# A transformer layer with a routed feed-forward: the shared expert's gate and up products as seven half-size products

## The chip, the cores and the metric

The kernel runs on one core of a Trainium2 chip. A core has five engines with queues of their own: TensorE (PE, matrix products into PSUM), VectorE (DVE), ScalarE (ACT), GpSimd (POOL) and SyncE (SP, which issues most transfers). They meet at semaphores. The metric is the device time of one execution in microseconds, the median of several runs.

## The reference

The input is 2 x 2048 tokens of width 512, treated as 4096 rows. Three blocks follow one another: an attention against two fixed weight matrices, a cross attention to 128 context rows, and a feed-forward with one shared expert and 32 routed experts, of which each token takes one. The change is in the shared expert:

```python
def _swiglu(x, gw, uw, dw):
    return jax.nn.silu(x @ gw) * (x @ uw) @ dw
...
x = hidden_states.reshape(-1, h)
shared_out = _swiglu(x, shared_gate_w, shared_up_w, shared_down_w)
logits = x @ gate_w
topk_ids = jnp.argmax(logits, axis=-1)
...
d = _grouped_mm(jax.nn.silu(g) * u, routed_down_w, tokens_per_expert)
inv = jnp.argsort(order)
routed_out = d[inv]
return (shared_out + routed_out).reshape(b, s, h)
```

Here `x` is 4096 x 512 (normalised rows), the gate and up weights are 512 x 1024, the down weights 1024 x 512.

## The kernel before

Products of fp32 precision are made of three passes on TensorE. `split` (line 88) cuts a value into a high half (a cast, line 93, on ScalarE unless told otherwise) and a low half (what is left, line 96, on VectorE or GpSimd), and `three` (line 162) gives the three pairs low-high, high-low and high-high. One product of a 128-row contraction is so three matmuls, each with its own weight load.

The stages follow in program order: `stage0` (attention), `stage1` (cross attention; its `finish` writes the sum x2, the normalised and transposed rows as high and low halves into the DRAM tensor `zT`, the gate logits and the scaled rows `xs`), `shared`, `routed`, and `overflow`, a loop for tokens that exceed the planned capacities. A scheduler orders each engine's instructions by priority (program order unless `later` moves it) and by a model of the times; tiles of one tag share a fixed number of slots, and a tile waits for a free one. Stages overlap where tiles and data allow.

`shared` works on tiles of 512 tokens (`t`, 8 of them) and on six of the eight blocks of 128 hidden columns (`HID`). `up(t, c)` makes gate and up of one block, 12 matmuls of 512 columns each (4 contraction blocks times 3) into one bank of PSUM each, then Silu on ScalarE, the product on VectorE, and the split of the hidden value. `down(t)` makes 4 x 6 x 3 = 72 matmuls into four banks, adds x2 and writes `out`; it is issued after the first block of the next tile. The weights of all six blocks are loaded and split once, by `shared_weights`, in the background of stage 1's end, and stay in 36 of the 48 slots of the pool W. The last two hidden blocks, called rest, have their own 12 slots and are worked in `routed` by `Rest`, in 16 blocks of 256 tokens between the experts' blocks.

`route` (called once, after the first tile) computes on VectorE which token goes to which expert's rows, and scatters the token numbers into the DRAM list `ids` with 32 indirect transfers from GpSimd's queue (line 719), each of which writes the same tensor and so waits for the one before it. Line 721 then reads the list back; `gather` in `routed` needs it.

`routed` loads each expert's gate, up and down weights (lines 897, 898), splits them into slots of W (gate and up, 16 + 16) and of the tags A and B (down), and works blocks of 256, 128 or 64 tokens.

Of the kernel before, what the change touches and what calls it, by code (L numbers as in the profile page):

```python
# [14 lines left out]
A = mybir.AluOpType  # L15
# [22 lines left out]
HID = 6  # L38
# [6 lines left out]
class Ctx:  # L45


    SLOTS = {"A": 8, "B": 8, "C": 5, "D": 4, "E": 4, "F": 8, "G": 4, "H": 3, "I": 2, "J": 2, "K": 2}

    def __init__(self, tc, stack):  # L50
        self.tc, self.nc = tc, tc.nc
        enter = stack.enter_context
        self.c = enter(tc.tile_pool(name="c", bufs=1))
        self.sm = enter(tc.tile_pool(name="sm", bufs=3))
        self.raw = enter(tc.tile_pool(name="raw", bufs=6))
        self.W = enter(tc.tile_pool(name="W", bufs=48))
        self.a = enter(tc.tile_pool(name="a", bufs=1))
        self.ps = enter(tc.tile_pool(name="ps", bufs=2, space=PSUM))
# [301 lines left out]
def stage1(g, x1, mask, kst, vst, gate, x2, zT, xs, ef, background):  # L360
# [143 lines left out]
    def finish(t):  # L504
# [13 lines left out]
        for i, v in enumerate(z):  # L518
            normalise(g, v[:], v[:], mv, rs, i)
        yield  # L520
        z2 = transposed(z, "z", "BBEF" if t < NT - 2 else "JJKK")
        for i in range(2):
            for c in range(2):
                nc.sync.dma_start(zT[i, :, 2 * c:2 * c + 2, t * 256:(t + 1) * 256], f32(z2[i][c][:]))
# [79 lines left out]
def route(g, ef, tab, tri, ids, plan, idx):  # L604
# [34 lines left out]


    oh = table("oh", bc(io, 1, E), bc(ef[:], 2, E), A.is_equal, tag="J")
    pos, cnt = ([g.tile("G", n, F32, (128, 16, E)) for _ in range(2)] for n in ("pos", "cnt"))
    for hf in range(2):
        for w, dst in ((0, pos), (1, cnt)):
# [3 lines left out]
            V.tensor_copy(dst[hf][:], o[:])  # L648
    for t in range(1, E):
# [3 lines left out]
        V.tensor_tensor(cnt[h][:, i, :], cnt[h][:, i, :], cnt[hp][:, ip, :], A.add)  # L653


# [4 lines left out]
    total(rank[:], table("gt", bc(key[:], 1, E), bc(key[:], 2, E), A.is_gt)[:])  # L660
    ro = table("ro", bc(io, 1, E), bc(rank[:], 2, E), A.is_equal, tag="J")
    base, cap, er = small("base"), small("cap"), small("er")
    total(base[:], table("wb", ro[:], bc(basec, 1, E), A.mult)[:])
    total(cap[:], table("wc", ro[:], bc(capc, 1, E), A.mult)[:])
    total(er[:], table("we", ro[:].rearrange("p e r -> p r e"), bc(io, 1, E), A.mult)[:])
    V.tensor_copy(plan[:, 0:E], er[:])


# [7 lines left out]
    V.tensor_copy(plan[:, 96:97], nov[:])  # L676
    ovs, ove = small("ovs"), small("ove")
    total(ovs[:], table("lt", bc(io, 2, E), bc(io, 1, E), A.is_gt, bc(over[:], 1, E), A.mult)[:])
    V.tensor_tensor(ove[:], ovs[:], over[:], A.add)
    for hf in range(2):  # L680
        te = small(f"te{hf}")
        total(te[:], table("le", bc(iota[:, 32 * hf:32 * hf + 32], 2, E), bc(ove[:], 1, E), A.is_ge)[:])
        V.tensor_scalar(te[:], te[:], float(E - 1), None, A.min)
        V.tensor_copy(plan[:, 32 + 32 * hf:64 + 32 * hf], te[:])


# [3 lines left out]
    for hf in range(2):  # L690
# [4 lines left out]
        past = g.tile("K", "past", F32, (128, 16, E))  # L695
        V.tensor_tensor(sel[:], pos[hf][:], capb, A.is_ge)
        V.tensor_tensor(past[:], sel[:], capb, A.mult)
        V.tensor_tensor(pos[hf][:], pos[hf][:], past[:], A.subtract)
        V.tensor_tensor(sel[:], sel[:], diffb, A.mult)
        V.tensor_tensor(sel[:], sel[:], baseb, A.add)  # L700
        V.tensor_tensor(sel[:], sel[:], oh[:, ts, :], A.mult)
        total(blk[:, ts], sel[:])
        V.tensor_tensor(pos[hf][:], pos[hf][:], oh[:, ts, :], A.mult)
        total(pt[:, ts], pos[hf][:])
    pi, hi = small("pi", I32), small("hi", I32)
# [7 lines left out]
    V.tensor_tensor(blk[:], blk[:], pt[:], A.add)  # L713
    dst, toki = small("dst", I32), small("toki", I32)
    V.tensor_copy(dst[:], blk[:])
    V.tensor_copy(toki[:], tok)
    flat = ids[:].rearrange("p (b o) -> (p b) o", o=1)
# [7 lines left out]
def shared_weights(g, wg, wu, wd):  # L725

    g.sw, g.rest = {}, {}
# [8 lines left out]
    g.sw["d"] = yield from weight_steps(g, wd[0:768, :], 6, 512, "sd")  # L736
    for name, w in (("g", wg), ("u", wu)):
# [4 lines left out]
        yield from split_steps(g, w[:, 768:1024], *o)  # L742
    g.rest["d"] = yield from weight_steps(g, wd[768:1024, :], 2, 512, "rd")


def shared(g, zT, x2, out, routing, rest):
    nc = g.nc
    NT = T // 512
    wg2, wu2, wd2 = (g.sw[z] for z in "gud")
    H = {}  # L750

    def up(t, c, z):
        o = []
        for nm, w2, tag in (("g", wg2, "P3"), ("u", wu2, "P2")):
            p = g.bank(tag, nm)
            n = 0
            for k in range(4):
                for w, y in three((w2, z)):
                    nc.tensor.matmul(p[:], part(w, k, c), y[k][:], start=n == 0, stop=n == 11)
                    n += 1  # L760
            o.append(p)
        s = g.tile("H", "s")
        nc.scalar.activation(s[:], o[0][:], AF.Silu)
        nc.vector.tensor_tensor(s[:], o[1][:], s[:], A.mult)  # L764
        hh, hl = g.tile("A", "hh", FR), g.tile("B", "hl", FR)
        split(g, hh[:], hl[:], s[:])
        H[t, c] = (hh, hl)

    def down(t):
        o = [g.bank(("P4", "P1")[s // 2], "d") for s in range(4)]  # L770
        for c in range(HID):
            h2 = H.pop((t, c))
            for s in range(4):
                for n, (w, y) in enumerate(three((wd2, h2))):
                    nc.tensor.matmul(o[s][:], y[:, s * 128:(s + 1) * 128], w[c][0], start=c == 0 and n == 0, stop=c == HID - 1 and n == 2)
        for s in range(4):
            rows = slice(t * 512 + s * 128, t * 512 + s * 128 + 128)
            b = g.tile("I", "b")
            nc.sync.dma_start(b[:], x2[rows, :])
            nc.vector.tensor_tensor(b[:], o[s][:], b[:], A.add)  # L780
            nc.sync.dma_start(out[rows, :], b[:])

    for t in range(NT):
        z = []
        for i in range(2):
            tag = ("EF", "CD")[t % 2][i]
            z.append([g.tile(tag, f"z{i}", FR) for _ in range(4)])
# [469 lines left out]
```

## Time and profile before

| | us |
|---|---|
| median of 3 runs | 2712.58 (2712.46 to 2713.4) |
| the profiled execution | 2710.05 |
| its span | 2708.3 |
| first matmul of the shared stage (line 759) | 1402.7 |
| last matmul of the shared stage (line 775) | 1819.8 |
| first matmuls of the rest and routed stage (line 827) | 1820.0 |

The span runs from the first to the last record of the profiled execution, and times in the views count from its start. The share of an engine's busy time is over the whole span. Matmuls overlap one another, and their ends are modelled, so the sum of their lengths is not time. The mean transfer rate per fortieth of the span lies between 32 and 191 GB/s up to the end of the shared stage and between 268 and 330 GB/s in most of the routed one.

### The profile page before, as it was taken

What the parts mean: (1) busy time and instruction counts of PE and PEld (TensorE: products, weight loads), DVE (VectorE), ACT (ScalarE), POOL (GpSimd) and SP (SyncE); (2) the same over time, 40 slices, a digit from 0 to 9 for tenths busy, and PEclk for the clock granted to TensorE, in tenths of its full rate; (3) what the DMA queues carried; (4) which work ended last, traced back from release to release, by engine and by line L of the source; (5) the groups of instructions that cost most, each with busy time, mean ns of one, the idle gap of its engine ahead of it and who ended that gap; (6) DMA issues with size and microseconds to landing.
All of it is one profiled execution on the core that took longest, in us unless ns stands there. A gap on an engine that the chain in (4) does not pass through costs nothing. (4 is left out here: it accounts for less than half of the span.)

```text
span 2708.3 us, 46790 instructions
## 1 busy us (share of the span) xinstructions
PE 2658.4 (98%) x14736; PEld 2293.1 (85%) x14736; DVE 1960.8 (72%) x4605; ACT 1802.8 (67%) x4012; POOL 953.9 (35%) x788
## 2 busy tenths in 40 slices
PE   7999999999999999999999999999999999999998
PEld 5878888887888999899988888888989898888886
DVE  7777777777777988888876722243777777778995
ACT  6788787888767777777774111133666777767884
POOL 5576565666643333333330130001122111212221
PEclk9999999999999999999999999999999999999999
DMA  4012122212121223222245323254888999999994
GB/s 151 32 63 83 59 67 80 77 43 82 34 82 33 80 76 114 95 88 79 85 145 191 98 94 106 86 170 113 268 281 277 287 300 292 300 276 287 330 325 130
DMA packets 237995, 396.64 MB, mean 146 GB/s; under 512 B 29377, under 2 KB 67281, under 8 KB 237745
## 3 DMA queue, kind: packets, MB, share of 16 engines
q1 hardware_dynamic: 223024, 366.45, 40.3%
q0 software_dynamic: 14720, 27.19, 5.1%
q8 instruction: 116, 1.90, 0.3%
q14 instruction: 135, 1.10, 0.1%
HBM read 311.67 MB, written 83.83 MB: 146 GB/s over the span
## 5 line engine op out<-in xcount | busy, mean ns | idle before, releaser
L96 DVE TENSOR_TENSOR rl<-raw,rh 128x512 fp32r<-128x512 f32 x768 | 488.6, 684 | 101.5 <-ACT rh L93 94.5
L93 ACT CAST rh<-raw 128x512 fp32r<-128x512 f32 x768 | 439.2, 621 | 121.9 <-DMA raw<-in_rg 76.5
L96 POOL TENSOR_TENSOR pl<-p,ph 128x512 fp32r<-128x512 f32 x320 | 411.0, 1295 | 269.7 <-ACT ph L93 217.0
L343 ACT ACTIVATE rl<-s 128x512 f32<-128x512 f32 x512 | 293.1, 604 | 39.5 <-PE s L339 33.6
L1043 POOL DMA_INDIRECT out_dram<-v,idx x46 | 100.5, 2185 | 430.0 <-ACT v L1041 352.2
L347 DVE TENSOR_TENSOR p<-s,rl 128x512 f32<-128x512 f32 x320 | 215.2, 683 | 41.7 <-ACT rl L343 39.3
L93 ACT CAST ph<-p 128x512 fp32r<-128x512 f32 x320 | 199.2, 626 | 63.6 <-DVE p L347 60.7
L452 ACT ACTIVATE e<-e,nm 128x128 f32<-128x128 f32 x512 | 199.2, 391 | 61.5 <-DVE nm L449 61.3
L455 POOL TENSOR_TENSOR e<-e,ri 128x512 f32<-128x512 f32 x128 | 133.5, 1043 | 243.7 <-DVE ri L453 126.5
L339 PE MATMUL s<-qh,kwl 128*128 128x512 f32 x512 | 205.7, 403 | 8.0 <-DVE p L347 4.0
L303 PE MATMUL o<-pl,vwh 128*128 128x512 f32 x512 | 202.4, 395 | 0.5 <-POOL pl L96 0.5
L303 PE MATMUL o<-ph,vwl 128*128 128x512 f32 x512 | 200.4, 393 | 0.9 <-ACT ph L93 0.9
L339 PE MATMUL s<-ql,kwh 128*128 128x512 f32 x512 | 200.4, 391 | 0.0
L339 PE MATMUL s<-qh,kwh 128*128 128x512 f32 x512 | 200.3, 391 | 0.0
L303 PE MATMUL o<-ph,vwh 128*128 128x512 f32 x512 | 199.7, 390 | 0.0
L347 DVE TENSOR_TENSOR s<-s,rl 128x512 f32<-128x512 f32 x192 | 133.4, 695 | 89.7 <-ACT rl L343 89.4
L909 POOL DMA_INDIRECT x<-xs,idx x46 | 55.1, 1198 | 351.6 <-DMA raw<-in_rd 172.1
L93 ACT CAST hh<-s 128x512 fp32r<-128x512 f32 x92 | 57.0, 620 | 166.4 <-DVE s L764 116.6
L426 PE MATMUL q<-yh,wql 128*128 128x256 f32 x512 | 149.3, 292 | 2.3 <-DVE v L485 2.1
L96 DVE TENSOR_TENSOR pl<-s,ph 128x512 fp32r<-128x512 f32 x192 | 131.2, 683 | 21.1 <-ACT ph L93 18.5
L426 PE MATMUL q<-yh,wqh 128*128 128x256 f32 x512 | 145.5, 284 | 0.0
L426 PE MATMUL q<-yl,wqh 128*128 128x256 f32 x512 | 144.8, 283 | 0.0
(303 smaller groups left out, 7745.0 us busy)
## 6 DMA issues: line engine op xcount, KB each, us to landing
raw<-in_rg SPq DMA_DIRECT2D x256, 256.0 KB, 5.4
raw<-in_ru SPq DMA_DIRECT2D x256, 256.0 KB, 4.9
raw<-in_rd SPq DMA_DIRECT2D x256, 256.0 KB, 5.2
z<-zT SPq DMA_DIRECT2D x128, 256.0 KB, 5.4
b<-x SPq DMA_DIRECT2D x64, 256.0 KB, 2.7
xt<-in_x SPq DMA_DIRECT2D x32, 256.0 KB, 3.8
x<-xt SPq DMA_DIRECT2D x32, 256.0 KB, 2.5
x<-b SPq DMA_DIRECT2D x32, 256.0 KB, 2.1
```

The costliest lines, as they stand in the source:

```text
L93: g.nc.scalar.copy(hi, src)
L96: (lo_engine or g.nc.vector).tensor_tensor(lo, src, f32(hi), A.subtract)
L303: nc.tensor.matmul(o[:], w, y[:], start=kt == 0 and n == 0, stop=kt == 15 and n == 2)
L339: nc.tensor.matmul(s[:], w, y[:], start=n == 0, stop=n == 2)
L343: m0 = nc.scalar.activation(r[:], s[:], AF.Relu)
L347: m1 = nc.vector.tensor_tensor(p[:], s[:], r[:], A.mult)
L426: nc.tensor.matmul(o[:, i, :], part(w, k, p), y[k // 2][:, k % 2, :], start=n == 0, stop=n == 11)
L452: nc.scalar.activation(e[:, hs], e[:, hs], AF.Exp, bias=nm[:, h:h + 1], scale=0.125, accum_out=su[:, h:h + 1])
L455: nc.gpsimd.tensor_tensor(e4, e4, ri[:].unsqueeze(2).to_broadcast([128, 4, 128]), A.mult)
L909: nc.gpsimd.indirect_dma_start(out=x[rows], out_offset=None, in_=xs, in_offset=bass.IndirectOffsetOnAxis(ap=idx[rows, b + j:b + j + 1], ax ...
L1043: nc.gpsimd.indirect_dma_start(out=out, out_offset=bass.IndirectOffsetOnAxis(ap=idx[rows, b + j:b + j + 1], axis=0), in_=v[rows], in_offse ...
```

## The change

The first 1024 tokens are worked as before, in two tiles of 512. From there on a group of 1024 tokens and a pair of hidden blocks is one step: the token halves, the halves of the contraction (256 each) and the two blocks form 2 x 2 matrices of blocks, for gate and for up, and seven products of halves (Strassen's scheme in Winograd's form) take the place of eight. The sums of token blocks (`S1` to `S4`) are formed on GpSimd from `zF`, the plain sum of high and low halves that stage 1 now writes too, and split again. The sums of weight blocks (`T1` to `T4`) are formed once per pair on GpSimd from weights that the host has laid out by blocks (`sgu`), split, and written to the DRAM tensor `wS`, from which later groups load them. The weights of gate and up are no longer resident after the first two tiles; each step loads those of the next.

Three PSUM tags with two banks each hold the seven products: product 1 is copied out to SBUF and product 2 added onto it in the same bank; 6, 7 and 4 share a bank, 5 and 3 another. VectorE joins them. The down product of a step runs in parts of six matmuls between the products of the next step (`between`), and adds onto `ACC`, a tile that holds x2 over the three pairs of a group. `route` has become a generator that advances between blocks and products. The rest weights are loaded in the last step instead of at the end of stage 1. W has 45 slots, C 6 and D 6. In `zT` the 256-token pieces of a group stand in another order (`place`), and in the last two pieces of stage 1 the normalised rows go to slots of W.

```diff
-HID = 6
+PAIRS = 3
...
-    SLOTS = {"A": 8, "B": 8, "C": 5, "D": 4, "E": 4, "F": 8, "G": 4, "H": 3, "I": 2, "J": 2, "K": 2}
+    SLOTS = {"A": 8, "B": 8, "C": 6, "D": 6, "E": 4, "F": 8, "G": 4, "H": 3, "I": 2, "J": 2, "K": 2}
...
-        self.W = enter(tc.tile_pool(name="W", bufs=48))
+        self.W = enter(tc.tile_pool(name="W", bufs=45))
...
+def place(t):
+    at = t // 4 * 4 + t % 2 * 2 + t % 4 // 2
+    return slice(at * 256, at * 256 + 256)
...
         for i, v in enumerate(z):
-            normalise(g, v[:], v[:], mv, rs, i)
+            if t >= NT - 2:
+                z[i] = g.W.tile([128, 512], F32, name="zn", tag="W")
+            normalise(g, z[i][:], v[:], mv, rs, i)
...
+        with later(g, 40):
+            for c in range(2 if t > 3 else 0):
+                v = g.tile("D", "zf", F32, (128, 2, 256))
+                nc.gpsimd.tensor_tensor(v[:], f32(z2[0][c][:]), f32(z2[1][c][:]), A.add)
+                nc.sync.dma_start(zF[:, 2 * c:2 * c + 2, place(t)], v[:])
...
+PRODUCTS = {1: (0, "A11", "B11"), 2: (0, "A12", "B21"), 3: (2, "S4", "B22"), 4: (1, "A22", "T4"),
+            5: (2, "S1", "T1"), 6: (1, "S2", "T2"), 7: (1, "S3", "T3")}
+TURN = (1, 6, 5, 7, 2, 4, 3)
+INPUTS = {"A11": "EEEE", "S2": "FFFF", "S1": "FFFF", "S3": "AAAA", "A12": "AAAA", "A22": "BBBB", "S4": "BBBB"}
...
+def sums(g, zF, G, out):
...
+        s3, s1, s2, s4 = a[1, 0], a[1, 1], a[0, 0], a[0, 1]
+        nc.gpsimd.tensor_tensor(s1[:], s1[:], s3[:], A.add)
+        nc.gpsimd.tensor_tensor(s3[:], s2[:], s3[:], A.subtract)
+        yield
+        nc.gpsimd.tensor_tensor(s2[:], s1[:], s2[:], A.subtract)
+        nc.gpsimd.tensor_tensor(s4[:], s4[:], s2[:], A.subtract)
...
+class Pairs:
...
+    def put(self, v, p=None, n=None):
+        g = self.g
+        hi, lo = g.piece("swh"), g.piece("swl")
+        split(g, hi[:], lo[:], v[:], g.nc.gpsimd)
+        if n is not None:
+            for i, x in enumerate((hi, lo)):
+                g.nc.sync.dma_start(self.wS[p, n - 1, i], f32(x[:]))
+        return hi, lo
...
+    def sums(self, p, w):
+        b12, b22 = self.raw(p, 1), self.raw(p, 3)
+        t3 = self.g.raw.tile([128, 512], F32, name="raw", tag="raw")
+        self.minus(t3, b22, b12)
+        w["T3"] = self.put(t3, p, 3)
+        yield
...
+    def steps(self, p, w, made):
+        if not made:
+            yield from self.sums(p, w)
+        for n in TURN:
+            b = PRODUCTS[n][2]
+            if b[0] == "B":
+                w[b] = self.put(self.raw(p, "11 12 21 22".split().index(b[1:])))
+            elif made:
+                w[b] = self.g.piece("swh"), self.g.piece("swl")
+                for i in range(2):
+                    self.g.nc.sync.dma_start(f32(w[b][i][:]), self.wS[p, int(b[1]) - 1, i])
+            yield
...
+def load_z(g, zT, SUM, G, name):
+    z = z_tiles(g, name)
+    for j in range(2):
+        if name[0] == "S":
+            split(g, z[j][0][:], z[j][1][:], SUM[name][j][:], g.nc.gpsimd)
+            continue
+        at = G * 1024 + (int(name[1]) - 1) * 512
+        for i in range(2):
+            g.nc.sync.dma_start(f32(z[j][i][:]), zT[i, :, (int(name[2]) - 1) * 2 + j, at:at + 512])
+    return z
...
+    def up(G, p, w, between):
+        banks = [[g.bank(tag, "gu") for _ in range(2)] for tag in ("P1", "P2", "P3")]
...
+        for n in TURN:
+            at, a, b = PRODUCTS[n]
+            for x in range(2):
+                o = banks[at][x]
+                for j in range(2):
+                    wj = [v[:, x * 256 + j * 128:x * 256 + j * 128 + 128] for v in w[b]]
+                    for m, (y, z) in enumerate(three((wj, [v[:] for v in Z[a][j]]))):
+                        nc.tensor.matmul(o[:], y, z, start=(at, x) not in begun, stop=j == 1 and m == 2, skip_group_check=True)
+                        begun.add((at, x))
+                if n == 1:
+                    P1[x] = g.tile("G", "p1")
+                    nc.scalar.copy(P1[x][:], o[:])
+                elif n == 6:
+                    U2[x] = g.tile("H", "u2")
+                    nc.vector.tensor_tensor(U2[x][:], o[:], P1[x][:], A.add)
+                elif n == 7:
+                    U3[x] = g.tile("I", "u3")
+                    nc.vector.tensor_tensor(U3[x][:], o[:], P1[x][:], A.add)
+                    nc.vector.tensor_tensor(U3[x][:], banks[2][x][:], U3[x][:], A.add)
...
+                elif n == 4:
+                    nc.vector.tensor_tensor(o[:], o[:], P1[x][:], A.add)
+                    gate_or_up(x, o[:], P1[0], 1, 0)
+                elif n == 3:
+                    nc.vector.tensor_tensor(o[:], o[:], U2[x][:], A.add)
+                    gate_or_up(x, o[:], U2[0], 0, 1)
+            between(a)
...
+    def down(G, p, w, half, s):
+        o = g.bank("P4", "d")
+        for c in range(2):
+            for n, (v, y) in enumerate(three(([z[:] for z in w[c]], H[G, p, half, c]))):
+                nc.tensor.matmul(o[:], y[:, s * 128:(s + 1) * 128], v, start=c == 0 and n == 0, stop=c == 1 and n == 2)
...
+        b = ACC[half, s]
+        nc.vector.tensor_tensor(b[:], o[:], b[:], A.add)
+        if p == PAIRS - 1:
+            nc.sync.dma_start(out[r, :], b[:])
...
+    for t in range(2):
...
+            plain_up(t, c, z)
+            if t == 0 and c > 0:
+                next(ahead, None)
+            if t == 1:
+                next(parts, None)
+            if (t, c) > (0, 1):
+                for _ in range(4):
+                    next(routing, None)
...
+    steps = [(G, p) for G in range(1, NG) for p in range(PAIRS)]
+    before, parts = [lambda s=s: plain_down(1, s) for s in range(4)], None
+    for n, (G, p) in enumerate(steps):
+        last = n + 1 == len(steps)
+        if p == PAIRS - 2 and G + 1 < NG:
+            parts = sums(g, zF, G + 1, SUM)
+        wn = {}
+        ahead = rest_weights if last else pairs.steps(steps[n + 1][1], wn, G > 1 or p == PAIRS - 1)
+        behind = down_weights(g, wd, p, w)
+        def between(a):
+            next(ahead, None)
+            if len(before) < 5:
+                next(behind, None)
+            if parts:
+                next(parts, None)
+            if p == PAIRS - 1 and G + 1 < NG:
+                Z[a] = load_z(g, zT, SUM, G + 1, a)
+            if before:
+                before.pop(0)()
+            next(routing, None)
+        up(G, p, w, between)
...
+    gu = np.stack([np.asarray(w)[:, :256 * PAIRS].reshape(2, 2, 128, PAIRS, 2, 128)
+                   for w in (L0_ffn_shared_gate_w, L0_ffn_shared_up_w)])
...
+        "sgu": arr(gu.transpose(4, 1, 5, 3, 0, 2, 6)).reshape(PAIRS, 4, 128, 512),
```

## The prediction

> **What bounds the kernel now.** I read the engine totals first, then TensorE's waits from the shared stage to the end, then the timeline inside that stage, because a total of pipelined matmuls can hide gaps.
>
> ```profile
> PE 2658.4 (98%) x14736; PEld 2293.1 (85%) x14736; DVE 1960.8 (72%) x4605; ACT 1802.8 (67%) x4012; POOL 953.9 (35%) x788
> ```
>
> ```profile
> PE g L759 <- ACT s L763: 1.7, 1, 1.7
> PE g L1000 <- DVE tl L96: 1.3, 4, 0.3
> PE d L945 <- ACT th L93: 1.0, 1, 1.0
> ```
>
> ```profile
> 1651.36 2.88 PE L759 MATMUL g<-z,sw 128*128 128x512 f32 x12
> ...
> 1654.08 2.88 PE L759 MATMUL u<-z,sw 128*128 128x512 f32 x12
> ...
> 1656.80 2.88 PE L759 MATMUL g<-z,sw 128*128 128x512 f32 x12
> ```
>
> TensorE (PE) is busy all the time, and from 1380 us to the end the waits that the second view lists (us in total, times, longest) sum to a few us; these three are its longest. So the end is set by the number of matmuls times their pace, and every one taken away should show. The three timeline rows give the pace: twelve matmuls of 512 columns start 2.72 us after the twelve before, twice running, so **0.2267 us each**. The groups of these lines say something else:
>
> ```profile
> L759 PE MATMUL u<-z,sw 128*128 128x512 f32 x576 | 140.1, 390 | 0.0
> L759 PE MATMUL g<-z,sw 128*128 128x512 f32 x576 | 139.5, 390 | 1.7 <-ACT s L763 1.7
> ```
>
> Their 390 ns is start to modelled end of one, with the next already running; 576 times 390 ns would be 225 us, and the busy time says 140. It is not what a removed matmul returns.
>
> The stage has room on the other engines, in two different stretches:
>
> ```profile
> 1534.00:1626.00 92.00, 92.00 (x408) 76.17 (x407) 20.66 (x30) 14.63 (x24) 32.09 (x33) 1.00 0.27 87
> 1626.00:1790.00 164.00, 164.00 (x725) 135.82 (x724) 39.46 (x58) 25.99 (x43) 0.00 (x0) 1.00 0.29 97
> ```
>
> After the two ends and the length the columns are PE, its weight loads, DVE, ACT and POOL, then clock, DMA share and GB/s. The clock is 1.00; VectorE is busy 22 to 24% of these stretches, ScalarE 16%, GpSimd 35% and then not at all. What occupies GpSimd in the first is a chain:
>
> ```profile
> 1533.61 1.20 POOL L719 DMA_INDIRECT ids<-small  x1 [85.21 <-DVE small L715]
> 1537.52 0.97 POOL L719 DMA_INDIRECT ids<-small  x1 [2.71 <-DMA ids<-small]
> ...
> 1621.49 0.96 POOL L719 DMA_INDIRECT ids<-small  x1 [1.44 <-DMA ids<-small]
> 1623.89 0.59 POOL L721 DMA_DIRECT2D idx<-ids  x1 [1.45 <-DMA ids<-small]
> ```
>
> The 32 scatters of the routing each wait for the landing of the one before, mostly 2.4 us a link, 90 us in all, with GpSimd's queue held in the gaps.
>
> **What the change removes.** A group of 1024 tokens takes, for a pair of blocks, 2 token halves x 2 blocks x 24 = 96 gate and up matmuls; seven products of 12 make 84. Three groups times three pairs: 9 x 12 = 108 fewer, all of 512 columns. The down product stays: 48 a pair and group, as before (576 over all tokens). So 1728 matmuls become 1620. By the rows 108 x 0.2267 = **24.5 us**. The Trainium skill has a rule on this (TensorE: Matmul & The Clock Gate, "Back-to-back issue gap"): a sustained stream of weight load and matmul at 512 columns runs at about 131 ns, an isolated gap at 216. By its sustained figure 14.1 us would come back. It doesn't fit this trace, where the stream is sustained and steps by 226.7, so I take the row.
>
> **What the nine new steps cost beside the matmuls.** A step (84 products, 48 down matmuls of the pair before) is 132 x 0.2267 = 29.9 us of TensorE. VectorE: 10 additions that join products (U2 2, U3 4, 2 each for products 4 and 3), 4 gate times up, 4 low halves of the hidden values, 8 output additions, 2 low halves of down weights: 28 at 0.684 us (line 96 mean) = 19.2 us. ScalarE: 2 copies of product 1, 4 Silu, 4 + 3 + 2 high halves, 15 at 0.62 = 9.3 us, with formed weight sums or token sums up to 14.3. GpSimd at 1.3 us (1295 ns, its line 96 row): 3 low halves of plain blocks; 8 for sums of weights formed; 8 for sums of tokens in a pair's step, 8 to split them in the next: at most 19 in a step, 24.7 us. Transfers: 8 tiles of kept sums, 3 plain blocks, 2 down weights of 256 KB, and at the end of two groups 12 token tiles and 8 outputs, 33 x 0.262 MB in 29.9 us = 289 GB/s; the routed stage holds 268 to 330 in most slices of the GB/s row. SyncE takes 5.32 us to issue eight such loads in the timeline, so 22 us for 33; its queue is in order, and a load that waits for a slot holds the token and x2 loads behind it, but each is asked for a step ahead of its use. All lie below the step's 29.9 us; cover gone, an overfull engine costs its excess only.
>
> Joins: a product bank is read while other banks are filled. The tightest distance is one product and one down part, 18 x 0.2267 = 4.1 us, against one or two VectorE operations, 0.7 to 1.4. I take 1 us for nine steps; ends 0 and 9 x 0.7 = 6.
>
> A second rule speaks against moving sums to GpSimd: a VectorE operation with two SBUF inputs contends with a GpSimd one that reads SBUF (the Trainium skill, SBUF — State Buffer, "Who interferes with whom"). The nearest row is the start of the kernel, where both split kw: VectorE takes 693 and 1184 ns there, against 684 alone. So half a microsecond a collision. By row and rule alike four such operations a step lose 2 us of VectorE's free 10.7, which TensorE doesn't see; in the plain part below it only delays the routing.
>
> **What is moved or squeezed, and where it could show.**
> - *Routing in pieces.* Its work is the same; VectorE was busy 83 of the 101 us up to 1534. About 19 GpSimd operations beside it add at most 10 us of collisions. The list is ready at 1624 and first used near 1797, so 170 us cover it.
> - *The scatter chain meets the sums on GpSimd.* The first seven-product step starts near 1510, where the plain tiles' 360th matmul ends in this trace; it has 84 + 72 matmuls (35 us), the next begin near 1545, 1575, 1605. The chain lies over them. In those 92 us GpSimd owes 11 + 19 + 11 = 41 operations, 53 us, plus 32 us of scatters: 85 of 92. One operation of 1.3 us fits each 1.44 us gap, so an alternating order takes 32 of the 41 and leaves 9 that stretch the chain, 9 x 1.3 = 12 us at its end. Ends: 0 and 12 (the other order is the rival D). I take 2.5, since the weight sums need only inputs and can start before the chain.
> - *45 weight slots for 48.* The routed stage holds 12 for the rest blocks; 33 instead of 36 serve gate and up, a whole expert being 32. It loses one and a half pairs of lead. A pair's split takes 0.7 us, an expert's gate pieces are used a whole up product (5.4 us) before the next expert's: most of the 32 experts have the slack, and the D and C tiles gain slots. Ends -1 and 8; I take 1.5, with the end of the stage in it: eight down parts of 1.36 us on two banks, each emptied by 0.7 us of VectorE that also splits expert weights.
> - *Stage 1.* 24 more GpSimd sums (29 us over 600, on an engine 38% busy there) and the tail where shared weights wait for slots: ends 0 and 6, I take 0.5. Two normalisations to other tiles cost the same.
> - *Stage 0*'s last three output weights wait for slots until its key weights are free; they are first used five steps into stage 1. Nothing.
>
> **Sum**, against the profiled execution's own 2710.05 us (span 2708.3): 2710.05 - 24.5 + 1 + 2.5 + 1.5 + 0.5 = 2691.1. The median of the runs shown lies 2.5 us above that execution, so **2693.5 us** on its scale.
>
> **Rivals.**
> - *A, forecast:* the pace holds and stalls stay under 10 us; 2687 to 2698. Chance 0.58.
> - *B, GpSimd late or slots short:* the upper ends of both come due, 12 + 8 us for 4; 2693.5 + 16 = 2709.5, at half that 2702. For it: 85 of 92 us. Against: it is one short stretch, and inputs are early. Chance 0.25 for 2698 to 2720, in which faster is 0.16, same 0.07, slower 0.02.
> - *C, more than forecast:* a removed matmul gives back its 390 ns, 42.1 us: 2710.05 - 42.1 + 2.5 = 2670.5; or the tails of stage 1 and the routed stage come to lie better than now by 3 us, 2685. The pace speaks against the first. Chance 0.05.
> - *D, slower:* GpSimd's queue is in order. If the scatters stand ahead of the weight sums of the second pair, due near 1553, TensorE idles until the chain passes at 1626: 73 us, 2712.6 - 24.5 + 73 = 2761. It decides from a stall of 24.5 us on, that is, some ten links of 2.4 us ahead of a sum already due. For it: the chain is written before those sums. Against: they can run in its gaps. Chance 0.12, spread over 2718 to 2761.
> - That the products don't shrink: the code counts 84 for 96; no chance given.
>
> A measurement of this kernel tells a change from none at about 0.2%, 5.4 us: faster is below 2707.2. Faster 0.58 + 0.16 + 0.05 = 0.79, same 0.07, slower 0.14. The range reaches from C's upper case, 2685, through B to 2713; 2687 to 2698 is A's own.
>
> **What would show it.** 14628 matmuls instead of 14736; the same 2.72 us for twelve; TensorE full in every window from 1510 to the routed stage, which begins some 24 us earlier; VectorE near 64% there, GpSimd near 80% in the first three steps, scatters and sums alternating. I'd be wrong if TensorE waits on a weight or token sum (line 96 on GpSimd) by more than 10 us, if the expert matmuls (lines 945 and 1000 here) wait for their weights, or if twelve matmuls no longer take 2.72.

## The result, and the profile after

The changed kernel takes 2722.22 us, median of 6 runs (2719.23 to 2724.48); the kernel before, in the same comparison, 2712.06 (2709.16 to 2713.4). The ratio is 1.0038, 95% interval 1.0025 to 1.0051: slower by 10 us, where 2693.5 was forecast. The profiled execution took 2720.02 us, its span is 2718.2; the one before took 2710.05, so these two also lie 10 us apart.

The page's row of engine totals for the kernel after (us, share of the span, instructions):

```profile
PE 2646.2 (97%) x14628; PEld 2277.5 (84%) x14628; DVE 2099.9 (77%) x4761; ACT 1852.7 (68%) x4111; POOL 1120.0 (41%) x911
```

The 108 matmuls are gone, 14628 are left. TensorE's timeline after, in the shared stage (start, length, what it is, and in brackets the idle time before it and who ended it):

```profile
1501.44 0.79 PE L917 MATMUL d<-sdl,hh 128*128 128x512 f32 x1 [6.71 <-DVE b L920]
1502.03 0.63 PE L917 MATMUL d<-sdh,hl 128*128 128x512 f32 x1
1502.46 0.63 PE L917 MATMUL d<-sdh,hh 128*128 128x512 f32 x1
...
1556.69 0.39 PE L951 MATMUL gu<-z,swl 128*128 128x512 f32 x1
1556.92 0.62 PE L951 MATMUL gu<-z,swh 128*128 128x512 f32 x2
1557.37 0.39 PE L951 MATMUL gu<-z,swl 128*128 128x512 f32 x1
...
1563.80 0.80 PE L951 MATMUL gu<-z,swl 128*128 128x512 f32 x1 [3.32 <-DVE u L961]
```

Three products' matmuls step by 0.68 us (1556.69 to 1557.37), 0.227 each: the pace is the forecast one, so the 24.5 us did come back. But there are pauses that the kernel before did not have, and after a long one the next matmuls step by 0.43 us (1502.03 to 1502.46), about half the pace. The largest waits of TensorE after, from 1450 to 1850 us (total, times, longest), then the busy time by stretch (columns as in the prediction):

```profile
PE d L917 <- DVE b L920: 6.7, 1, 6.7
PE gu L951 <- DVE u L961: 3.3, 1, 3.3
PE d L983 <- DVE acc L989: 3.1, 3, 1.5
PE pt L1180 <- DMA x<-xs,idx: 2.6, 1, 2.6
```

```profile
1453.00:1510.00 57.00, 50.26 (x208) 40.08 (x209) 47.92 (x107) 19.44 (x34) 32.51 (x25) 0.91 0.58 196
1510.00:1600.00 90.00, 85.08 (x365) 68.73 (x364) 72.98 (x109) 26.34 (x46) 47.80 (x38) 0.98 0.61 208
1600.00:1700.00 100.00, 96.89 (x425) 79.21 (x424) 67.62 (x95) 34.46 (x61) 62.31 (x54) 1.00 0.62 203
1700.00:1800.00 100.00, 100.00 (x443) 82.81 (x442) 68.36 (x106) 36.85 (x67) 23.92 (x19) 1.00 0.65 220
```

TensorE is full from 1700 to 1800 only. Until then VectorE stands 68 to 84% busy and GpSimd 53 to 62%, together; the granted clock falls to 0.91 where the longest pause lies.

To see where the time went I summed, over the matmul records of each profiled execution, what lies between two starts beyond the pace of a matmul of that width. The first 100 matmuls of the shared stage, which still mix with the end of stage 1, have a row of their own:

| us beyond the pace | before | after | after − before | forecast |
|---|---|---|---|---|
| stage 0 | 26.0 | 29.0 | +3.0 | 0 |
| stage 1 | 21.5 | 25.4 | +3.9 | +0.5 |
| shared, first 100 matmuls | 2.1 | 0.8 | −1.3 | |
| shared, the others | 0.1 | 28.4 | +28.3 | +1 +2.5 and part of 1.5 |
| rest and routed | 9.5 | 10.3 | +0.8 | part of 1.5 |

34.7 us are lost against 24.5 gained, which makes the 10; the forecast had 5.5 of loss. Most of it is in the shared stage. What VectorE and GpSimd do at its longest pause and at the second one, VectorE's timeline first:

```profile
1488.42 1.24 DVE L668 TENSOR_TENSOR pos<-pos,cnt 128x32 f32<-128x32 f32 x1
1489.59 1.33 DVE L669 TENSOR_TENSOR cnt<-cnt 128x32 f32<-128x32 f32 x1
...
1495.90 0.19 DVE L668 TENSOR_TENSOR pos<-pos,cnt 128x32 f32<-128x32 f32 x1
1496.01 0.18 DVE L669 TENSOR_TENSOR cnt<-cnt 128x32 f32<-128x32 f32 x1
...
1558.14 5.00 DVE L97 TENSOR_TENSOR dwl<-raw,dwh 128x512 fp32r<-128x512 f32 x1 [2.97 <-ACT dwh L94]
```

```profile
1488.32 1.30 POOL L799 TENSOR_TENSOR zs<-zs 128x512 f32<-128x512 f32 x1
1489.56 1.31 POOL L97 TENSOR_TENSOR z<-zs,z 128x512 fp32r<-128x512 f32 x1
1490.81 1.30 POOL L800 TENSOR_TENSOR zs<-zs 128x512 f32<-128x512 f32 x1
1492.05 3.77 POOL L97 TENSOR_TENSOR z<-zs,z 128x512 fp32r<-128x512 f32 x3
...
1557.60 1.30 POOL L828 TENSOR_TENSOR raw<-raw 128x512 f32<-128x512 f32 x1
1558.86 1.29 POOL L97 TENSOR_TENSOR swl<-raw,swh 128x512 fp32r<-128x512 f32 x1
1560.11 1.26 POOL L828 TENSOR_TENSOR raw<-raw 128x512 f32<-128x512 f32 x1
1561.34 1.25 POOL L97 TENSOR_TENSOR swl<-raw,swh 128x512 fp32r<-128x512 f32 x1
```

The routing's additions of 32 columns take 0.18 us, but 1.2 to 1.33 while GpSimd forms the sums of token blocks: each ends with a GpSimd operation. Once GpSimd has finished, at 1495.8, they take 0.18 again. The low half of a down weight at 1558.14, 0.68 us elsewhere, takes 5.00 us: it lasts through four GpSimd operations that follow one another without a gap. Why the small additions get in after one operation of such a row and this one only after four, no run shows. Between 1450 and 1820 us 31 VectorE operations are longer by 33.6 us in all; before, from 1450 to 1800, none was.

The groups of two of these lines tell which operations are hit (duration in ns: shortest, median, longest). The routing's additions before, the same after, and the output additions after:

```profile
L652 DVE TENSOR_TENSOR pos<-pos,cnt x31: 181/192/193, 1474.7 to 1487.1; 128x32 f32<-128x32 f32 x31
```

```profile
L668 DVE TENSOR_TENSOR pos<-pos,cnt x31: 177/192/1239, 1475.9 to 1501.6; 128x32 f32<-128x32 f32 x31
L989 DVE TENSOR_TENSOR acc<-d,acc x72: 673/683/692, 1583.2 to 1840.5; 128x512 f32<-128x512 f32 x72
```

An output addition reads one input from PSUM (`d`). 17 of the 72 begin while a GpSimd sum is running, and none is longer than 0.69 us. In this stage only operations with both inputs in SBUF were stretched.

### The profile page after: what moved, and what is told of

Read it like the earlier page. It is cut to its first block, busy times and chain, and to the rows that moved or that the text cites. A ratio compares the mean times of both kernels' runs of the same rounds, so it can differ in the third digit from the quotient of the medians.

```text
span 2718.2 us, 47549 instructions
## 1 busy us (share of the span) xinstructions
PE 2646.2 (97%) x14628; PEld 2277.5 (84%) x14628; DVE 2099.9 (77%) x4761; ACT 1852.7 (68%) x4111; POOL 1120.0 (41%) x911
## 5 line engine op out<-in xcount | busy, mean ns | idle before, releaser
L1307 POOL DMA_INDIRECT out_dram<-v,idx x46 | 108.1, 2351 | 467.5 <-ACT v L1305 376.4
L951 PE MATMUL gu<-z,swh 128*128 128x512 f32 x504 | 158.0, 392 | 0.0
L97 DVE TENSOR_TENSOR pl<-s,ph 128x512 fp32r<-128x512 f32 x192 | 131.1, 683 | 21.5 <-ACT ph L94 18.9
```

The lines of the kernel that those rows point to most:

```text
L97: (lo_engine or g.nc.vector).tensor_tensor(lo, src, f32(hi), A.subtract)
L951: nc.tensor.matmul(o[:], y, z, start=(at, x) not in begun, stop=j == 1 and m == 2, skip_group_check=True)
L1307: nc.gpsimd.indirect_dma_start(out=out, out_offset=bass.IndirectOffsetOnAxis(ap=idx[rows, b + j:b + j + 1], axis=0), in_=v[rows], in_offse ...
```

## The experiments

Three theories were set against each other. *Port*: VectorE operations with two SBUF inputs wait for GpSimd's sums, and what stands behind them in VectorE's queue is late for TensorE. *Load* (called *queue* where it is about the order of a queue): VectorE or SyncE has too much to do in this stretch anyhow. *Slots*: weight slots and the scatter chain make the operands late. In runs 1 to 4 they carry the letters P, L and W. Ratios are to the kernel before, measured beside each run on the same chip; its own median lies between 2710.4 and 2712.8 from one group of runs to the next, so runs of different groups (1 to 4, 5 to 8, 9 and 10, 11 and 12, and the changed kernel itself) compare by their ratios, of which 0.001 is 2.7 us.

**1. All sums on VectorE.** Four token sums, the weight differences and all their low halves:

```diff
-        nc.gpsimd.tensor_tensor(s1[:], s1[:], s3[:], A.add)
+        nc.vector.tensor_tensor(s1[:], s1[:], s3[:], A.add)
...
-        split(g, hi[:], lo[:], v[:], g.nc.gpsimd)
+        split(g, hi[:], lo[:], v[:])
```

> All tensor operations that the shared stage's new steps give to GpSimd (sums of weight blocks and of token blocks, low halves of both) are on VectorE. Theory P (shared read port: a VectorE operation with two SBUF inputs waits until the GpSimd operation that is running, and any that follows without a gap, is done; VectorE's in-order queue passes it on to TensorE): no stretched VectorE operation is left after 1460 us, the 6.9 us and 3.5 us pauses of TensorE go, with the slow clock after them; against that VectorE takes over some 100 operations of 0.68 us, about 70 us over 330. Time 2708 to 2714. Rival L (VectorE is simply too full in the first steps, whoever works beside it): it gets fuller, so slower than 2722, near 2735. Rival W (weight slots and the scatter chain on GpSimd hold things up): the chain no longer delays sums, so 2716 to 2720, but the two long pauses stay.

2711.68 us (12 runs), ratio 1.0005 [0.9997, 1.0014]: 10.5 us below the changed kernel by the medians, 9 by the ratios, although VectorE has 99 more operations. One stretched operation is left (0.5 us in place of 33.6). This is inside the port theory's range and outside both others'. But the profiled execution took 2715.82, 4 us above the median, and its shared stage still lost as much beyond the pace as the changed kernel's (28 against 29 us): waits for the output additions (6.8 us) and for low halves of weights (5.2) stand in the place of the collisions. So the time speaks for the theory; the trace shows the collisions gone, not the gain.

**2. The routing at once**, after the blocks of the first plain tile, instead of in pieces:

```diff
-            if (t, c) > (0, 1):
-                for _ in range(4):
-                    next(routing, None)
+        if t == 0:
+            run(routing)
```

> The routing is issued in one piece after the first plain tile, as before the change, instead of in pieces between blocks and products; everything else as changed. P: its small operations finish before most of the token sums run on GpSimd, so fewer are stretched and the 6.9 us pause goes, the 3.5 us one (a down weight's low half against four GpSimd operations in a row) stays: 2712 to 2717. L: the routing's load is out of the first steps, so both pauses go: 2706 to 2712. W: the scatter chain starts earlier and is over sooner, the pauses after 1590 us shrink by 3 us: 2718 to 2720.

2719.14 us, ratio 1.0032 [1.0022, 1.0042]: 3 us back by the medians, 1.5 by the ratios, which the intervals don't tell from none. That is less than the port theory's range and inside the slots theory's. The trace shows why: in this run, too, the scheduler had put much of the routing beside the token sums. 32 VectorE operations are stretched, by 32.0 us, and a pause of 5.7 us stays at 1492. It did not separate what it was meant to.

**3. No token sums.** The four additions leave their inputs as they are:

```diff
-        nc.gpsimd.tensor_tensor(s1[:], s1[:], s3[:], A.add)
...
-            split(g, z[j][0][:], z[j][1][:], SUM[name][j][:], g.nc.gpsimd)
+            g.nc.scalar.copy(z[j][0][:], SUM[name][j][:])
+            g.nc.sync.dma_start(f32(z[j][1][:]), zT[1, :, j, G * 1024:G * 1024 + 512])
```

> Left out: the four sums of token blocks and their low halves on GpSimd (16 operations a group); the tiles are loaded and cast as before and the low halves come straight from memory, so slots, casts and VectorE's work stay. P: no GpSimd operation runs beside the routing's 62 small operations between 1477 and 1497 us; they take 0.18 us each, the 6.9 us pause and its slow clock go (9 us), some of the later ones too: 2709 to 2714. L: VectorE's own work is the same, so both long pauses stay: 2720 to 2723. W: GpSimd's queue is shorter by 48 operations, the pauses after 1590 us (5 us) go: 2716 to 2718.

2707.64 us, ratio 0.9990 [0.9981, 0.9999]. The pause of 6.9 us at 1494 is gone, 9 stretched operations and 10.5 us remain. Better than expected by 1.4 us. A new pause of 5.9 us ends at 1557: behind a hidden block's low half that took 5.70 us beside GpSimd's weight sums. The run also takes 48 operations out of GpSimd's queue, for which the slots theory had expected 2716 to 2718.

**4. One more kind of sum on GpSimd**, the low halves of the down weights:

```diff
-        split(g, w[c][0][:], w[c][1][:], raw[:])
+        split(g, w[c][0][:], w[c][1][:], raw[:], g.nc.gpsimd)
```

> Only the low halves of the down weights (two a step, both inputs in SBUF) go from VectorE to GpSimd. P: the 5.0 us operation that waited through four GpSimd operations is gone, with the 3.5 us pause and its slow clock (5 us) and most of the 1.6 us one near 1597: 2715 to 2717; the 6.9 us pause stays. L: VectorE loses 18 operations of 0.68 us over 330 us: 1 us at most. W: GpSimd gets 18 more operations in its fullest stretch, so 0 to 6 us slower.

2730.95 us, ratio 1.0078 [1.0061, 1.0095]: 9 us slower by the medians, 11 by the ratios, where the port theory expected a gain; the slots theory had the sign (0 to 6 us slower), not the size. It took away the operation that had been hit at 1558, and others were hit in its place: the low half of a hidden block took 5.71 us at 1618.7, a gate times up 5.37 us at 1722.7; pauses of 4.5 and 7.7 us follow these two. So the victim is whichever operation with two SBUF inputs comes up while GpSimd's operations run without a gap. That more of them make longer rows, and these the loss, fits the trace, but the run does not separate it from a fuller GpSimd queue.

**5. The kernel before with the new slots.**

```diff
-    SLOTS = {"A": 8, "B": 8, "C": 5, "D": 4, "E": 4, "F": 8, "G": 4, "H": 3, "I": 2, "J": 2, "K": 2}
+    SLOTS = {"A": 8, "B": 8, "C": 6, "D": 6, "E": 4, "F": 8, "G": 4, "H": 3, "I": 2, "J": 2, "K": 2}
...
-        self.W = enter(tc.tile_pool(name="W", bufs=48))
+        self.W = enter(tc.tile_pool(name="W", bufs=45))
```

> The kernel before with only the change's buffer counts: 45 weight slots for 48, and 6 of C and 6 of D for 5 and 4; every product stays plain. It asks whether the slots are what makes stages 0 and 1 some 7 us longer in the changed kernel (its pauses there: 29.0 and 25.4 us against 26.0 and 21.5). Slots theory: these two stages take on most of the 7 us, so 2714 to 2718 us. Port theory (the sums of token blocks on GpSimd in stage 1 do it): the slots cost 0 to 2 us, 2710 to 2712 us.

2715.37 us against 2712.81, ratio 1.0010 [1.0002, 1.0018]. By the medians the slots cost 2.6 us, between the theories' 0 to 2 and 4 to 8. In the profiled execution stages 0 and 1 have 28.0 and 24.9 us beyond the pace, 5.4 of the 6.9 us by which the changed kernel's exceed those before. That execution lies 5.3 us above the profiled one before and the medians only 2.6 apart, so up to half of the 5.4 may be the spread between executions.

**6. No sums in stage 1.**

```diff
-                nc.gpsimd.tensor_tensor(v[:], f32(z2[0][c][:]), f32(z2[1][c][:]), A.add)
-                nc.sync.dma_start(zF[:, 2 * c:2 * c + 2, place(t)], v[:])
+                nc.sync.dma_start(zF[:, 2 * c:2 * c + 2, place(t)], f32(z2[0][c][:]))
```

> The changed kernel with the sum of high and low half in stage 1 left out: the high half alone goes to the sums' array, by a DMA of the same size, so that the low half is left out of the token sums later. 24 GpSimd additions of 512 columns less. Port theory: those sums stretch VectorE's small operations of stage 1; 2 to 5 us come back there, 2717 to 2720 us. Slots theory: nothing comes back, 2721 to 2723 us, and stage 1 keeps its pauses of about 25 us. The pauses from 1450 us on stay in both.

2739.31 us, ratio 1.0094 [1.0079, 1.0109]: both theories missed by 16 us and more. 24 GpSimd operations less in stage 1, and stage 1 had 31.1 us beyond the pace, not less. In the shared stage, whose sums are the same in number, two low halves of down weights now took 7.65 us (at 1615.18) and 7.10 (at 1623.35); 30 stretched operations made 41.9 us. So the loss seems to depend on how the two queues happen to lie, and an edit that shifts them can cost more than the work it removes. For stage 1 itself it says nothing in favour of the sums as a cause.

**7. Token sums on VectorE, weight sums on GpSimd** (the token part of edit 1 alone).

> The changed kernel with the sums of token blocks and their low halves on VectorE; the sums of weights and their low halves stay on GpSimd. Port theory: the 6.9 us pause at 1494 and its slow clock go (about 9 us, as with all sums on VectorE), the pause behind the 5.00 us operation at 1558 and the two smaller ones stay (5 to 7 us): 2713 to 2717 us. If VectorE's load were the limit, sparing it the weight sums would help: below 2711.7 us, the time with all sums on VectorE. Slots theory: 2720 to 2723 us.

2719.06 us, ratio 1.0022 [1.0016, 1.0029]: above the expected range, and 4 us below the changed kernel by the ratios. The pause at 1494 is gone, as said. Another comes, in TensorE's timeline of this run; GpSimd's timeline shows what stands before it:

```profile
1562.10 0.80 PE L951 MATMUL gu<-z,swl 128*128 128x512 f32 x1 [6.91 <-POOL swl L97]
```

```profile
1554.96 1.27 POOL L828 TENSOR_TENSOR raw<-raw 128x512 f32<-128x512 f32 x1 [1.05 <-DMA raw<-in_sgu]
1558.54 0.99 POOL L750 DMA_INDIRECT ids<-small  x1 [2.32 <-DMA ids<-small]
1559.56 1.28 POOL L828 TENSOR_TENSOR raw<-raw 128x512 f32<-128x512 f32 x1
1560.77 1.28 POOL L97 TENSOR_TENSOR swl<-raw,swh 128x512 fp32r<-128x512 f32 x1
```

The low half that TensorE waits for stands behind a scatter that waits 2.3 us for the one before, and behind a difference that isn't needed yet. This is the place and mechanism of rival D, at the price of one link instead of 73 us. How much of the pause it makes is open: in run 1, with these sums on VectorE, low halves of weights were late there too, by 5.2 us.

**8. All sums on VectorE and several waits taken away**: edits 1 and 2, `zs` loaded a step ahead, and `U2` in a tile of tag J.

> The changed kernel with all sums on VectorE, the whole routing at once within the first block of plain products (as in the run of routing in one), the token blocks of the sums loaded one step ahead of their first sum, and the second product's saved tile in a buffer that the routed stage's gather does not wait for. Queue theory (what is left once the collisions are gone are waits of VectorE's queue and of two loads: 2.6 us at 1548, 2.6 in two pieces at 1560, 2.6 at 1577, 2.5 at 1820, and about 2 us of slow clock): 2700 to 2705 us, below the kernel before. Load theory (VectorE's 77% is itself the limit, so that the sums cost it what GpSimd saved): 2709 to 2713 us, and the pauses come back elsewhere between 1450 and 1700.

2715.97 us, ratio 1.0009 [1.0001, 1.0018]: by the ratio level with edit 1 alone (1.0005), the intervals overlap. The queue theory's 2700 to 2705 is refuted: the three added edits brought nothing that shows. In the profiled execution (2720.6, the slowest of the 13) TensorE waits 4.7 us for a low half of a weight on VectorE near 1558, behind a difference that waited for a raw block's load. Four edits at once don't tell what each did.

**9 and 10. Loads ahead on SyncE**, once with the sums on GpSimd, once with them on VectorE. After the traces of 7 and 8 the raw weight blocks were suspect: their loads stand on SyncE behind stores of `wS` that wait for the low halves. `keep` holds these stores, one step later than before.

```diff
         t3 = self.g.raw.tile([128, 512], F32, name="raw", tag="raw")
+        b11, b21 = self.raw(p, 0), self.raw(p, 2)
         self.minus(t3, b22, b12)
-        w["T3"] = self.put(t3, p, 3)
+        w["T3"] = self.put(t3)
         yield
-        b11 = self.raw(p, 0)
         self.minus(b12, b12, b11)
-        w["T1"] = self.put(b12, p, 1)
+        w["T1"] = self.put(b12)
+        self.keep(p, w, 3)
...
         a = PRODUCTS[n][1]
+        if n == 7:
+            run(ahead)
         Z[a] = load_z(g, zT, SUM, 1, a)
```

> The changed kernel with its sums still on GpSimd, but another order on SyncE's queue: the four raw blocks of a pair are loaded before the first difference is made, the sums' stores to DRAM go one step later, and what is left of the first pair's weights is loaded before the token blocks that wait for the last plain block. Queue theory (the weights come late because their loads stand behind stores that wait for GpSimd): the pauses between 1540 and 1600 (3.5, 1.6, 1.2 us and their slow clock) go, 2713 to 2717 us. Port theory: the stretched VectorE operations stay or move with GpSimd's phase, in all some 25 to 45 us of VectorE, and the time stays at 2718 to 2726 us.

> All sums on VectorE, as in the earlier run with 2711.7 us, and the order on SyncE's queue of the run with loads ahead. Queue theory: the two pauses for late low halves of weights (2.6 us at 1548, 2.6 us in two pieces at 1560) and their slow clock go, 2705 to 2708 us, below the kernel before. Load theory (VectorE's own amount of work makes them): 2710 to 2713 us, with pauses of the same length in the same place.

On GpSimd 2725.32 us, ratio 1.0050 [1.0036, 1.0064]; on VectorE 2707.96 us, ratio 0.9989 [0.9983, 0.9996]. Measured side by side, the place of the sums makes 17.4 us. The order alone did not help, as the port theory expected; with the collisions gone the time came to the upper end of the queue theory's range. VectorE's timeline with the sums on GpSimd:

```profile
1607.51 7.48 DVE L97 TENSOR_TENSOR dwl<-raw,dwh 128x512 fp32r<-128x512 f32 x1 [0.88 <-PE d L990]
1614.91 0.68 DVE L996 TENSOR_TENSOR acc<-d,acc 128x512 f32<-128x512 f32 x1
1615.51 5.89 DVE L97 TENSOR_TENSOR dwl<-raw,dwh 128x512 fp32r<-128x512 f32 x1
```

The first of these lasted through six GpSimd operations in a row. The output additions (`acc`), which free the down product's two banks, stand behind these two. One stretch of both runs shows the exchange; on GpSimd first, then on VectorE:

```profile
1600.00:1700.00 100.00, 94.95 (x407) 77.63 (x406) 73.39 (x92) 32.53 (x58) 60.43 (x52) 0.97 0.61 206
```

```profile
1600.00:1700.00 100.00, 100.00 (x442) 82.78 (x442) 81.88 (x132) 36.49 (x63) 21.25 (x22) 1.00 0.71 241
```

With 40 more operations VectorE is 8.5 us busier in these 100 us and does all of it in time; TensorE is full. Over the shared stage the loss beyond the pace falls by 18 us from run 9 to run 10, so here the traces show the gain that the times show. This version is 3.1 us faster than the kernel before beside it (2711.08). What it still waits for in the shared stage, from TensorE's waits with the sums on VectorE:

```profile
PE gu L958 <- DVE swl L97: 6.6, 5, 2.6
PE g L910 <- ACT s L914: 2.0, 1, 2.0
PE pt L1188 <- DMA x<-xs,idx: 1.7, 1, 1.7
```

Low halves of the first pairs' weights are late by 6.6 us: their raw loads start at 1540.9, on SyncE behind output rows of the plain blocks. The pauses near 1548 and 1560, which the order was to end, stayed (2.7, 2.0 and 1.5 us); between the two traces the later ones fell: that at 1691 (3.2 us) went, that at 1577 went from 2.8 to 1.2. So the queue theory's number came out and its mechanism did not. Run 1's trace is also of an execution 4 us above its median, so what the order gained on VectorE is not settled.

**11. The same order, token sums on VectorE, weight sums on GpSimd.**

> The order on SyncE's queue of the two runs before, token sums and their low halves on VectorE, weight sums and their low halves on GpSimd. It lies between these two (2725.3 with all sums on GpSimd, 2708.0 with all on VectorE) and shares their 17.4 us between the two kinds. Port theory: the token sums' collisions with the routing (about 7 us with slow clock) go, the weight sums' with low halves of down weights stay: 2713 to 2719 us. If GpSimd's queue (its sums behind the scatters, which wait 1.4 us each) makes the weight sums late, the pauses that remain are released by GpSimd and not by a stretched VectorE operation. Load theory: below 2708.

2717.56 us, ratio 1.0019 [1.0012, 1.0026], in the port theory's range, and by the ratios about halfway between runs 9 and 10: token sums and weight sums have some 8 us each. The longest pause, 6.2 us, is released by GpSimd, not by a stretched operation (stretched are 13, by 11.6 us). That does not make GpSimd's queue the cause: in run 10 low halves of these weights were late by 6.6 us without it. How the weight sums' part divides between collisions and queue stays open.

**12. A tile that the gather does not wait for.**

```diff
-                    U2[x] = g.tile("H", "u2")
+                    U2[x] = g.tile("J", "u2")
```

> The run with all sums on VectorE and loads ahead (2708.0 us), with the saved tile of product 6 in one of two buffers that the shared stage leaves free, so that the routed stage's second and third gather need not wait for the last pair's joins. If the late gather (1.7 us of pause at the start of the routed stage, and its slow clock) is that wait: 2705 to 2707 us. If the gather is late for another reason: 2707.5 to 2709 us.

2730.82 us, ratio 1.0065 [1.0051, 1.0079]: 23 us slower than run 10 by the medians, 21 by the ratios. In the profiled execution (2737.53, the slowest of the five) TensorE pauses 19.3 us at 1673, for an output addition. SyncE's timeline of this run, and GpSimd's:

```profile
1664.52 0.37 SPq L815 DMA_DIRECT2D raw<-in_sgu  x1
1687.45 0.33 SPq L874 DMA_DIRECT2D raw<-in_sd  x1
1687.88 0.38 SPq L998 DMA_DIRECT2D out_dram<-acc  x1
1688.36 0.37 SPq L994 DMA_DIRECT2D acc<-x  x1
```

```profile
1685.18 0.96 POOL L750 DMA_INDIRECT ids<-small  x1 [1.44 <-DMA ids<-small]
1687.59 0.59 POOL L752 DMA_DIRECT2D idx<-ids  x1 [1.45 <-DMA ids<-small]
```

SyncE's timeline of run 10 in the same place:

```profile
1666.68 2.97 SPq L994 DMA_DIRECT2D acc<-x  x2
1686.58 0.33 SPq L815 DMA_DIRECT2D raw<-in_sgu  x1
```

In both one weight load on SyncE waits until the last scatter has landed, for 22.5 us here and 16.9 in run 10. In run 12 the x2 rows of three output tiles (`acc<-x`) stand behind it, so their additions are late and the down product's banks stay full; in run 10 the last of them are issued just before it and TensorE sees nothing. The pause of 3.2 us at 1691 in run 1 ends with such a row too. The traces of the changed kernel and of runs 1, 8 and 11 have one such load as well, and so has the kernel before (an expert's weights, issued at 1757, when the scatters had long landed); where the scheduler puts it decides. Why it is tied to the scatters I did not find out, and no version without the tie was tried. TensorE's wait for the gather (1.7 us) is not in this run's list, but one of 2.0 us for ScalarE stands in its place, and with everything 20 us later the run does not show whether the tile was what the gather waited for.

## Why the prediction was wrong

- **Removed matmuls, 24.5 us: right.** The count and the pace are as said.
- **The failed step is the price of a collision**: "So half a microsecond a collision. By row and rule alike four such operations a step lose 2 us of VectorE's free 10.7, which TensorE doesn't see". The row behind it (693 and 1184 ns against 684) caught a single collision: the first of the two was over before GpSimd's began, and the second met the rest of one GpSimd operation. Here GpSimd's follow one another, and a collision costs a whole one of them or several: 1.0 to 1.15 us for most of the routing's small additions, 4.3 us at 1558 in the changed kernel, up to 7.0 (7.65 − 0.68) in other runs. In sum the 31 collisions cost VectorE 33.6 us, not far from what the prediction allowed (nine steps of 2 us, and at most 10 in the plain part). So it was not the sum that failed but the size of the single one, and with it "which TensorE doesn't see": free time over a whole step does not help a matmul that waits behind one operation of 5 us. The Trainium skill's warning (SBUF — State Buffer, "Who interferes with whom") was the right one, and I had weighed it; its size I took from a row where no queue of such operations existed.
- **The second half of that step failed too**: "only delays the routing", with 170 us of cover. It was not the routing that mattered but what stands behind it in VectorE's queue: the addition of a plain output row (`b`, line 920), which TensorE waited for 6.7 us. I had named the work that is hit, and not the queue behind it. The three pauses that follow stretched operations (6.9, 3.5, 1.6 us) and the slow matmuls right after the first two (3.7 us) make about 16 of the 28.3 us. Moving the sums to VectorE returned 9 us by the ratios, and 17.4 with loads ahead; this also relieves GpSimd's queue, so not all of it need be collisions.
- **Scatter chain and GpSimd, +2.5 (0 to 12):** 85 of 92 us were expected on GpSimd; it was 53 to 62% busy. The chain did lengthen (its end moved from 1624 to 1702), and rival D did not come true in the changed kernel. In runs 7 and 11 TensorE waited 6.9 and 6.2 us for a weight sum on GpSimd, behind a scatter in both; how much of that is the chain is open (above). In run 12 the chain cost up to 19 us by way of SyncE, a place that no rival had.
- **45 slots, +1.5 (−1 to 8):** right in size, 2.6 us by the medians of run 5 (the interval is 0.5 to 4.9), but in the wrong place. The loss is in stages 0 and 1, for which I had written "Nothing" and 0.5, and where the changed kernel lost 6.9; the routed stage lost 0.8.
- **Joins, +1 (0 to 6):** one row speaks for them, 3.1 us in three waits for `acc`; the change's products cannot run without them, and no run separated them. In run 10, with collisions gone, 17.7 us remain in the shared stage beyond the pace, 15.5 more than before, where all the terms of the forecast for this stage come to 4 or 5. So a second step failed, "All lie below the step's 29.9 us": an engine whose sum fits into a step was still late with single operands. By TensorE's waits 6.6 us are late low halves of weights, 2.0 a Silu where stage 1 ends (1.7 before), 1.7 the gather; half-pace matmuls cost 2.1. What would remove them no run shows.
- **Chances:** the time lies 0.38% above before, in the "slower" that had 0.14. It fell among D's cases by its size, for another reason.

## What to carry to other kernels

Work moved to GpSimd is not free for VectorE when both read SBUF: count what its rows of back-to-back operations do to the VectorE operations beside them, and then ask who waits behind those in VectorE's in-order queue. Here VectorE doing all the work itself was 9 to 17 us faster than sharing it. And when an engine's queue is the margin, compare versions on the chip: a small edit that shifted the queues (runs 6 and 12) moved the time by 15 to 23 us, close to the whole gain in matmuls.

## What the hardware showed beyond that

- A VectorE operation with two SBUF inputs can wait through several GpSimd operations, not only the one running: 5.00 us beside four of 1.25 to 1.30 us, 7.48 beside six in run 9. Beside the same kind of row additions of 32 columns waited for one, and the 72 output additions, with one input in PSUM, for none.
- In the shared stage of the changed kernel pauses of 2.5, 3.5 and 6.9 us were followed by six to eight matmuls that step by 0.43 instead of 0.227 us (1502.03, 1502.46, 1502.88), those of 1.4 to 1.6 us by none; after the pause of 2.5 us five or six went at the full pace first. The granted clock of the stretch with the longest pause reads 0.91.
- The cost of moving work off GpSimd is smaller than its operation count: from run 9 to run 10 VectorE takes on 99 operations that step by about 0.6 us, and its busy total rises by 11.8 us only, 2111.6 to 2123.4, because the stretched ones go.
